# Layer 0 of a four-layer graph network: first product with seven products for eight, adjacency turned by whole groups, engine order from a table

## The chip, the core and the metric

The kernel runs on one core of a Trainium2 chip. A core has a matrix engine (TensorE, PE in the profile), a vector engine (VectorE, DVE), a scalar engine (ScalarE, ACT), a general engine (GpSimd, POOL) and a queue processor (SyncE, SP) that issues most DMAs. PE reads SBUF and writes the eight banks of PSUM. DVE and ACT move results from PSUM to SBUF. All data here are 32-bit floats. The metric is the device time of one execution in microseconds, as the median of several.

## What is computed

There are 128 graphs of 64 nodes with 256 features. Four layers follow one another, each with a residual sum and a normalisation over the features. Layer 0 is the part that the change rewrites:

```python
GROUPS = [list(range(25)), [0, 1, 2, 3, 4, 5, 6, 7, 8], [0, 9, 10, 11, 12, 13, 14],
          [6, 7, 8, 12, 13, 14], [3, 4, 5, 9, 10, 11]]

def _graph_conv(x, adj, W, b):
    A = adj + jnp.eye(n)
    deg = jnp.sum(A, axis=-1)
    dinv = jnp.where(deg == 0, 0.0, deg_safe ** (-0.5))
    norm_adj = dinv[:, :, None] * A * dinv[:, None, :]
    support = jnp.einsum('bnd,de->bne', x, W)
    out = jnp.einsum('bnm,bme->bne', norm_adj, support) + b
    return jax.nn.relu(out)

for g, idx in enumerate(GROUPS):
    h = _graph_conv(x[:, idx], adj[:, idx][:, :, idx], W1[g], b1[g])   # 256 -> 512 features
    out_g = _graph_conv(h, adj[:, idx][:, :, idx], W2[g], b2[g])       # 512 -> 256
    fused = fused.at[:, idx].add(norm_w[g] * out_g)
x = layernorm(x + fused)
```

Layers 1 and 2 are a graph convolution and a polynomial of the normalised adjacency. Layer 3 is a gated recurrent cell over five steps; it fills most of the run and the change leaves it as it is.

## The kernel before

Layer 0 is cut into 16 units. A unit holds up to four tiles; a tile holds the chosen nodes of so many graphs that its rows fit 128 partitions (14 graphs of group 1, 16 of group 2, 21 of groups 3 and 4, 5 of group 0). The groups come in the order 1, 2, 3, 4, 0: units 0 to 2, 3 and 4, 5 and 6, 7 and 8, 9 to 15. A full unit has 448 to 504 columns; the last of a group has fewer (144, 264, 264 and 200).

For each unit, in stages:

- `load0` loads `a` (rows of the adjacency) and `xg` (rows of x) for the unit, one DMA per tile and run of nodes.
- `prep` adds the identity, sums degrees, takes the root on POOL (`inv_sqrt`, a power instruction, L144), scales, spreads each row into a block-diagonal 126x126 matrix A0 (L467), has PE turn it into the bank pT (L475), and DVE scales the other side while it moves it to SBUF as AT (L480).
- `aggregate` multiplies xg by AT (pa, L492), and ACT copies the result to ag0 (L498).
- `hidden` is the first product: ag0 times W1 in four output blocks of 128, two matmuls each over the whole width of the unit (ph, L508), and four ReLUs on ACT (L512).
- `support` multiplies by W2, four matmuls of 256 columns a tile (ps, L524), copied by ACT.
- `add` multiplies by AT again (po, L546), ACT takes the ReLU with the group's weight (L550), and DVE adds the sum over groups: into F for groups 1 to 4, from F for group 0.
- `finish`, for group 0's units alone, has PE turn the sums back to rows (pse, L581), DVE adds them to xg (L586), normalises, and SP stores the rows.

The nodes outside group 0 (25 to 63) need only a normalisation; `others` does it for four nodes at a time in between. Layers 1 and 2 of the first two chunks of graphs (`mid`, a generator called `early`) are laid into the last turns of the loop by a list of places. Weights that layer 3 needs are loaded by POOL's queue at turn 4 (L750 to L760); their products, `folds` (L644), begin layer 3's preparation.

PE's order is the program order, written by hand through the loop over `i`, in which unit i's support, unit i+1's aggregate and first product, and unit i-1's add stand side by side. The order of the other engines in layer 0 is found by a scheduler, with hints (`issue_after`, `high_priority`). Banks of PSUM rotate through two pools of five and three. From layer 3 on, all engines follow hand-written order strings. There the gate products already use a scheme of seven products in place of eight (`Gates`): the two-by-two block product is made from seven half-width ones, with sums of the moving side taken on POOL (L817 to L819), a running bank that ACT copies between products (L857), and DVE additions from PSUM (L861).

Of the kernel before, what the change touches and what calls it, by code (L numbers as in the profile page):

```python
# [27 lines left out]
NP = CB // 2  # L28
# [36 lines left out]
WARM = 4  # L65

# [26 lines left out]
def gnn_stack(  # L93
# [305 lines left out]
    with ExitStack() as c0:  # L399
        w0 = c0.enter_context(tc.tile_pool(name="w0", bufs=1))  # L400
        work = c0.enter_context(tc.tile_pool(name="work0", bufs=1))
        W1 = w0.tile([128, NG, 2, HID], F32, name="W1")
        W2 = w0.tile([128, NG, 4, D], F32, name="W2")
# [6 lines left out]
        def load0(i, after=None):  # L410
# [5 lines left out]
            a = work.tile([TR, 4, NJ], F32, name="a", bufs=3)  # L416
            xg = work.tile([TR, 4, D], F32, name="xg", bufs=6)
# [7 lines left out]
            for rows, t, b, f in runs:  # L425
                qa[t % len(qa)].dma_start(a[rows, t, :w], adj[b, f, 0:w])
# [55 lines left out]

        def aggregate(i):
# [17 lines left out]
        def hidden(i):  # L501
# [3 lines left out]
            for e in range(4):  # L505
                p = psum0("ph")[:, : u.cols]
                for k in range(2):
                    nc.tensor.matmul(  # L508
                        p, W1[:, u.g, k, e * 128 : (e + 1) * 128], ag0[:, k, : u.cols], start=k == 0, stop=k == 1
                    )  # L510
# [4 lines left out]

        def support(i):
            u = UNITS[i]
            hg, s2 = HG.pop(i), []
            for v in range(0, len(u.tiles), 2):
                p = psum0("ps").rearrange("p (t d) -> p t d", t=2)  # L520
                ts = range(v, min(v + 2, len(u.tiles)))
                for t in ts:
                    for e in range(4):
                        nc.tensor.matmul(  # L524
                            p[: u.rows[t], t - v, :], hg[:, e, u.off[t] : u.off[t] + u.rows[t]], W2[:, u.g, e, :],
                            start=e == 0, stop=e == 3,
                        )
                sv = work.tile([TR, 2, D], F32, name="s2", bufs=4)
# [6 lines left out]
            S2[i] = s2  # L535

        def add(i):
# [4 lines left out]
            z = work.tile([128, 2, 512], F32, name="z", bufs=2)  # L542
            for k in range(2):
# [8 lines left out]
                )  # L552
            if u.g < 2:
# [16 lines left out]

        def finish(i):
# [3 lines left out]
            for v in range(0, len(u.tiles), 2):  # L575
                p = psum0("pse").rearrange("p (t d) -> p t d", t=2)
                ts = range(v, min(v + 2, len(u.tiles)))
                for t in ts:
                    r = u.rows[t]
                    for k in range(2):  # L580
                        nc.tensor.transpose(  # L581
                            p[:r, t - v, k * 128 : (k + 1) * 128], z[:, k, u.off[t] : u.off[t] + r], ident
                        )
                r = u.rows[v]
                if u.rows[ts[-1]] == r:
                    nc.vector.tensor_add(xg[:r, v : v + len(ts), :], p[:r, : len(ts), :], xg[:r, v : v + len(ts), :])  # L586
                else:
                    for t in ts:
                        r = u.rows[t]
                        nc.vector.tensor_add(xg[:r, t, :], p[:r, t - v, :], xg[:r, t, :])  # L590
            for ts, _, r, _ in u.same:
                layernorm(xg[:, ts], n=ts.stop - ts.start, r=r)
            for t, (b, nb) in enumerate(u.tiles):
                nc.sync.dma_start(xa[b // XP][b % XP : b % XP + nb], xg[: u.rows[t], t, :])
# [6 lines left out]

        def others(i):

            with tc.issue_after(evictions[-1].ins):
                layernorm(XO[i], n=XO[i].shape[1])

        def store_others(i):
            t = XO.pop(i)
            nc.sync.dma_start(xb[:, NP * i : NP * i + t.shape[1], :], t)

# [20 lines left out]
        def load_first(g):  # L631
            nc.sync.dma_start(W1[:, g], w1[g].rearrange("(k p) e -> p k e", p=128))

        def load_second(g):
            nc.sync.dma_start(W2[:, g], w2[g].rearrange("(k p) e -> p k e", p=128))

        load_first(1)

# [10 lines left out]
        early = both(mid(0, True), mid(1, True))  # L649

        places = [(1, 1), (1, 2), (2, 1), (2, 2), (2, 2), (3, 1), (3, 2), (3, 2)]
        places += [(4, 0), (4, 0), (4, 1), (4, 2), (4, 2), (5, 1), (5, 2), (5, 2)]

        def early_stage(i, place):
            for _ in range(places.count((i - g0, place))):
                next(early)
# [4 lines left out]

        g0 = next(i for i, u in enumerate(UNITS) if u.g == 0)
        for i in range(-2, NU + 1):
            if i >= 0:
                stage(load0, i + 3)
            stage(add, i - 1)
            if i:
                stage(aggregate, i + 1)
            early_stage(i, 0)
            stage(support, i)  # L670
            if not i:
                aggregate(1)
            if i == NU:
                folds = [products(0, q) for q in range(3)]
            stage(finish, i - 1, g0)
            early_stage(i, 1)
# [5 lines left out]
            else:  # L682
                stage(prep, i + 2)
                stage(hidden, i + 1)
            if i == -2:
# [4 lines left out]
                load0(2, powers[0])  # L690
                load_first(2)
            elif i == -1:
                load_second(2)
                load_first(3)
                for ks in (slice(3, 5), slice(0, 1)):
                    nc.sync.dma_start(block0[:, ks], c_block0[:, ks])
            elif i == 0:
                load_second(3)
            elif i < 5:
                (load_first, load_second)[(i - 1) % 2]((4, 0)[(i - 1) // 2])  # L700
            early_stage(i, 2)
            for f, j in ((store_others, i - 1), (others, i), (load_others, i + 2)):
                for o in range(10):
                    if min(o + 1, 9) == j:
                        f(o)
            if i == 0:

                with tc.issue_after(evictions[-1].ins):
                    nc.vector.memset(F, 0.0)
# [31 lines left out]
            elif i == 4:  # L741
# [6 lines left out]
                with tc.issue_after(powers[-1].ins):  # L748
                    for q in range(3):
                        nc.gpsimd.dma_start(ih[:, q], wihT[:, q * D : (q + 1) * D].rearrange("(k p) e -> p k e", p=128))  # L750
                    for l in range(L):
                        if l:
# [538 lines left out]
```

## Time and profile before

| what | us |
|---|---|
| median of 3 runs | 2125.28 |
| range of the runs | 2124.78 to 2125.33 |
| the profiled execution | 2125.68 |
| its span, first to last instruction | 2123.7 |
| PE busy in the span | 2102.9 |
| layer 0 (to the start of the folds) | 293.5 |
| folds and preparation of layer 3 | 32.5 |
| from the first gate product | 1797.7 |

The span is what the profile's instructions cover; the execution's own time is 2 us more. The page gives busy time by engine, the waits name who released an engine after idle time, the windows give the busy time of all engines in a stretch (columns: PE, PEld for weight loads, DVE, ACT, POOL, then the granted clock, the share of the DMA engines and GB/s), and the timeline gives start, length, engine, line and operation of merged runs of instructions. An fp32 matmul shows as two records, a transpose on PE as one.

### The profile page before, as it was taken

The page shows a single profiled execution, that of the slowest core. Times are in us where ns is not written, and L with a number is a line of the kernel's source. Part 1 is how long each engine was busy: PE and PEld are TensorE (multiplying, and loading weights), DVE is VectorE, ACT ScalarE, POOL GpSimd, SP SyncE. Part 2 cuts the span into 40 slices and gives each one's busy share as a digit, 9 for nine tenths or more (in the row PEclk, how much of TensorE's full clock was granted, in tenths as well). Part 3 has the DMA queues.
Part 4 walks back from the last instruction along what each step waited for, and adds up shares of the span by engine and source line. Part 5 has one row for each costly group of instructions (what it writes and reads, how often), then busy time and mean ns, then how long its engine had stood idle before and what let it go on. Part 6 is the DMA issues. An engine that isn't in the chain of part 4 may idle for free.

```text
span 2123.7 us, 31527 instructions
## 1 busy us (share of the span) xinstructions
PE 2102.9 (99%) x10738; PEld 1820.6 (86%) x10738; DVE 1661.1 (78%) x3849; ACT 978.9 (46%) x2006; POOL 594.8 (28%) x638
## 2 busy tenths in 40 slices
PE   9999999999999999999999999999999999999997
PEld 6777788888888888888888888888889888888886
DVE  3345666887988798788978898879887997888776
ACT  3333334445444454444544454445444454445453
POOL 3411122232323223222323332223232332223322
PEclk9999999999999999999999999999999999999999
DMA  6642110223321242223321342233312421233121
GB/s 167 178 135 63 33 44 21 55 60 75 85 70 41 68 97 65 50 56 80 90 54 40 75 100 59 56 72 79 80 41 60 95 75 40 60 65 93 47 56 40
DMA packets 522060, 149.81 MB, mean 71 GB/s; under 512 B 488734, under 2 KB 516924, under 8 KB 521900
## 3 DMA queue, kind: packets, MB, share of 16 engines
q1 hardware_dynamic: 516996, 142.58, 27.8%
q0 software_dynamic: 2192, 4.80, 1.0%
q8 instruction: 85, 1.39, 0.3%
q10 hardware_dynamic: 2712, 0.42, 0.1%
q14 instruction: 75, 0.61, 0.1%
HBM read 82.70 MB, written 65.01 MB: 70 GB/s over the span
## 4 chain that ended last, share of the span: by engine, by line
PE 86%; DVE 10%; issue 1%; DMA 1%; ACT 0%; SPq 0%; POOL 0%; DVEq 0%; POOLq 0%; ACTq 0%
PE parz L837 22%; PE pdrz L837 12%; PE pan L837 11%; PE pa L254 8%; PE pdn L837 5%; PE pbrz L837 5%; PE pd L333 5%; PE ps L524 5%; PE ph L508 4%; PE pbn L837 3%; DVE NI L995 1%; PE pa L492 1%; PE pp L314 1%; DVE NI L996 1%; PE po L546 1%
## 5 line engine op out<-in xcount | busy, mean ns | idle before, releaser
L938 ACT ACTIVATE RZ<-RZ,brz 128x256 f32<-128x256 f32 x474 | 214.7, 501 | 167.5 <-DVE RZ L861 166.8
L837 PE MATMUL parz<-Th,WHH 128*128 128x256 f32 x960 | 288.7, 382 | 3.1 <-ACT c L857 3.1
L817 POOL TENSOR_TENSOR Ta<-agg 128x512 f32<-128x512 f32 x80 | 103.7, 1296 | 662.4 <-ACT agg L256 662.3
L837 PE MATMUL parz<-Ta,V 128*128 128x256 f32 x960 | 285.5, 379 | 0.0
L857 ACT COPY c<-parz 128x512 f32<-128x512 f32 x240 | 139.0, 579 | 269.1 <-PE parz L837 268.2
L857 ACT COPY c<-pan 128x512 f32<-128x512 f32 x237 | 138.4, 584 | 183.9 <-PE pan L837 183.7
L953 ACT ACTIVATE NI<-NI,bih 128x256 f32<-128x256 f32 x316 | 149.2, 504 | 156.6 <-DVE NI L996 156.6
L837 PEld LDWEIGHTS parz<-Th,WHH 128*128 128x128 f32 x960 | 179.5, 190 | 35.5 <-ACT c L857 12.5
L837 PEld LDWEIGHTS parz<-Ta,V 128*128 128x128 f32 x960 | 182.4, 190 | 24.8
L170 POOL TENSOR_TENSOR rs<-ve,mhalf 128x4 f32<-128x4 f32 (+2 forms) x65 | 68.3, 1052 | 370.7 <-DVE ve L163 318.7
L817 POOL TENSOR_TENSOR Th<-hn 128x512 f32<-128x512 f32 x64 | 81.6, 1275 | 315.2 <-DVE hn L960 304.4
L958 DVE TENSOR_TENSOR RZ<-hn,NI 128x256 f32<-128x256 f32 x252 | 133.9, 532 | 34.8 <-ACT NI L953 34.4
L959 DVE TENSOR_TENSOR RZ<-RZ 128x256 f32<-128x256 f32 x316 | 150.9, 478 | 10.7
L861 DVE TENSOR_TENSOR NI<-pdn,c 128x512 f32<-128x512 f32 x158 | 108.1, 684 | 58.8 <-ACT c L857 55.3
L996 DVE TENSOR_TENSOR NI<-NI 128x256 f32<-128x256 f32 x237 | 137.9, 582 | 8.2
L837 PE MATMUL pan<-Ta,V 128*128 128x256 f32 x474 | 144.1, 385 | 0.2 <-ACT c L857 0.2
L837 PE MATMUL pan<-Th,WHH 128*128 128x256 f32 x474 | 141.0, 379 | 0.0
L861 DVE TENSOR_TENSOR RZ<-pdrz,c 128x512 f32<-128x512 f32 x160 | 109.6, 685 | 37.3 <-PE pdrz L837 26.0
L995 DVE SCALAR_TENSOR_TENSOR NI<-NI,bhh,RZ 128x256 f32<-128x256 f32 x237 | 129.1, 545 | 6.3 <-ACT RZ L938 1.4
L254 PEld LDWEIGHTS pa<-A,h 128*128 128x128 f32 x1024 | 124.5, 192 | 4.8 <-issue 1.5
L256 ACT COPY agg<-pa 128x512 f32<-128x512 f32 x160 | 93.6, 586 | 73.1 <-PE pa L254 72.2
L254 PE MATMUL pa<-A,h 128*128 128x128 f32 x1024 | 124.9, 275 | 1.4 <-DMA h<-hb 1.4
(228 smaller groups left out, 4716.8 us busy)
## 6 DMA issues: line engine op xcount, KB each, us to landing
hb<-flip SPq DMA_DIRECT2D x184, 256.0 KB
h<-hb SPq DMA_DIRECT2D x624, 64.0 KB
out_dram<-xt SPq DMA_DIRECT2D x30, 256.0 KB
hT<-hb SPq DMA_DIRECT2D x112, 64.0 KB
W<-in_w_dram SPq DMA_DIRECT2D x10, 512.0 KB
xt<-xb SPq DMA_DIRECT2D x32, 156.0 KB
xo<-in_x_dram SPq DMA_DIRECT2D x9, 512.0 KB
xb<-xo SPq DMA_DIRECT2D x9, 512.0 KB
```

What stands on the lines that cost most here:

```text
L254: nc.tensor.matmul(p[:, q * 128 : (q + 1) * 128], src(q, k), m[:, q, :], start=True, stop=True)
L333: nc.tensor.matmul(p[:, h, :], ag[:, k, q * 128 : (q + 1) * 128], W[:, k, :], start=k == 0, stop=k == 1)
L817: nc.gpsimd.tensor_sub(t[:, 0:2, :], a[:, :, H:], a[:, 0, :].rearrange("p (s n) -> p s n", s=2))
L837: nc.tensor.matmul(bank[:, g, :], w[:, q, i - 1, :], rhs, start=i in (1, 2, 5) and g == 0 and m == 0, stop=m == len(side) - 1, skip_group_ ...
L857: nc.scalar.copy(c, self.a)
L861: nc.vector.tensor_add(v, self.b if i == 2 else self.d, self.copies.pop({7: 7, 2: 1, 3: 6}[i]))
L938: nc.scalar.activation(v, self.g.a[:, q, :] if i == 4 else v, AF.Sigmoid, bias=brz[:, 2 * q + j : 2 * q + j + 1])
L953: nc.scalar.activation(n, n, AF.Tanh, bias=bih[:, 4 + j : 5 + j])
L958: nc.vector.tensor_sub(d, self.hT[:, j, f], n)
L959: nc.vector.tensor_mul(d, d, z)
L995: nc.vector.scalar_tensor_tensor(n[:, j, f], h, bhh[:, 4 + j : 5 + j], r[:, j, f], op0=ALU.add, op1=ALU.mult)
L996: nc.vector.tensor_add(n[:, j, f], i, n[:, j, f])
```

## The change

Seven things change, all in layer 0.

1. From unit 3 on, `hidden7` makes the first product with seven products of half the width for eight, as the gates do. `factors0` makes the sums of W1 on POOL, once per group; three sums of ag0 are made on POOL per unit; bank a is copied by ACT after products 1, 6 and 7; DVE adds copies to the banks b and d; ACT takes the ReLU in halves.
2. From unit 3 on, the adjacency is not turned by PE tile by tile. Whole graphs are loaded, 32 graphs on each of four bands of partitions; `norm_group` takes degrees and roots for a whole group, scales, turns 32x32 blocks with DVE, scales the other side and stores the result to DRAM; `load_turned` loads a unit's rows, and `spread_out` writes AT with one DVE product by the block mask.
3. For units 10 to 13 the sums are turned by DVE in 32x32 blocks (`turn_sum`), go through DRAM, and come back as rows (`finish_turned`).
4. The normalisations are cut into pieces (`pieces_of_norm`) that are called one by one.
5. From unit 2 on, ACT, DVE and POOL follow program order too, and the order of stages is a line of `ORDER0` per turn. Letters stand for stages (A aggregate, P add on PE, F the sum over groups, S a support tile, X spread, L loads, digits the seven products, b g d c their evictions, q a piece of what is waiting, e a piece of layers 1 and 2).
6. W1 and W2 are held for two groups at a time instead of all five, xg has five buffers instead of six.
7. Layer 3's weights are loaded three DMAs a turn from turn 5 on, instead of all at turn 4; F is cleared by POOL instead of DVE.

The core of the diff:

```diff
+ORDER0 = """
+P A S q L 1 X 2 F 6 5 q 7 g S q 4 d 3 b c S S
+A S 1 q q L q X q 2 5 q q 6 q S 7 P q S 4 q g q 3 q q S F b c d
+q q A L P 1 S q S 6 2 q X 5 q q q 7 S S g F q b 4 q q 3 d c
...
+        def norm_group(g):
+            n, o = len(GROUPS[g]), 0
+            S = AS[len(nts) % 2]
+            nts[g] = []
+            degrees(g)
+            deg, s, r = (roots[:, v, max(g - 1, 0)] for v in range(3))
+            nc.vector.scalar_tensor_tensor(s, deg, 0.0, deg, op0=ALU.is_equal, op1=ALU.add)
+            powers.append(nc.gpsimd.tensor_tensor(r, s, mhalf[:, :1].to_broadcast([128, 32]), ALU.pow))
+            for _ in range(WAITS):
+                yield
+            nc.vector.scalar_tensor_tensor(s, deg, 0.0, r, op0=ALU.not_equal, op1=ALU.mult)
+            d = s[:, :, None]
+            for f, m in RUNS[g]:
+                nc.vector.tensor_mul(S[:, :, f : f + m], AL[:, :, f : f + m], d.to_broadcast([128, 32, m]))
+            yield
+            nc.vector.transpose(AU.rearrange("p b n -> p (b n)"), S.rearrange("p b n -> p (b n)"))
+            yield
+            for f, m in RUNS[g]:
+                nc.vector.tensor_mul(S[:, :, o : o + m], AU[:, :, f : f + m], d.to_broadcast([128, 32, m]))
+                o += m
+            for f, m in RUNS[g]:
+                nt = dram.tile([B, m, n], F32, name=f"nt{g}{f}")
+                for v in range(4):
+                    nc.sync.dma_start(
+                        nt[32 * v : 32 * v + 32].rearrange("b j i -> j b i"), S[32 * v + f : 32 * v + f + m, :, :n]
+                    )
...
+                    with tc.high_priority():
+                        last = nc.vector.tensor_mul(
+                            AT[:r, ts, o : o + nb * m].rearrange("p t (b n) -> p t b n", n=m),
+                            a[:r, ts, None, c : c + m].to_broadcast([r, w, nb, m]),
+                            block0[:r, None, k, o : o + nb * m].rearrange("p t (b n) -> p t b n", n=m)
+                            .to_broadcast([r, w, nb, m]),
+                        )
...
+        def factors0(g):
+            w = work.tile([128, 4, 2, 128], F32, name="w7", bufs=2)
+            v = W1[g].rearrange("p k (u j e) -> p k j u e", u=2, j=2)
+            nc.gpsimd.tensor_add(w[:, 1], v[:, 0, 1], v[:, 1, 1])
+            nc.gpsimd.tensor_sub(w[:, 3], v[:, 0, 0], v[:, 0, 1])
+            nc.gpsimd.tensor_sub(w[:, 2], w[:, 1], v[:, 0, 0])
+            nc.gpsimd.tensor_sub(w[:, 0], v[:, 1, 0], w[:, 2])
...
+        def hidden7(i):
+            u = UNITS[i]
+            a = AG.pop(i)
+            c = u.cols // 2
+            t = work.tile([128, 4, 256], F32, name="t7", bufs=1)
+            nc.gpsimd.tensor_sub(t[:, 0:2, :c], a[:, :, c : 2 * c], a[:, 0, : 2 * c].rearrange("p (s n) -> p s n", s=2))
+            nc.gpsimd.tensor_sub(t[:, 2, :c], a[:, 1, c : 2 * c], t[:, 0, :c])
+            nc.gpsimd.tensor_sub(t[:, 3, :c], a[:, 1, :c], t[:, 2, :c])
...
+            def product(k):
+                n = {2: "b", 5: "d", 3: "d"}.get(k, "a")
+                if k in (1, 2, 5):
+                    banks[n] = psum0("ph")[:, : 2 * c].rearrange("p (u n) -> p u n", u=2)
...
+                for p in range(2):
+                    nc.tensor.matmul(
+                        banks[n][:, p, :], F7[u.g](k, p), rhs, start=k in (1, 2, 5) and p == 0, stop=p == 1,
+                        skip_group_check=True,
+                    )
+                if k in (1, 6, 7):
+                    copies[k] = work.tile([128, 2, 256], F32, name="c7", bufs=3)[:, :, :c]
+                    with tc.high_priority():
+                        nc.scalar.copy(copies[k], banks["a"])
+
+            def evict(k):
+                j, f, of = {2: (0, 0, 1), 7: (1, 1, 7), 4: (1, 0, 0), 3: (0, 1, 6)}[k]
+                o = hv[:, j, :, f * c : f * c + c]
+                if of:
+                    with tc.high_priority():
+                        nc.vector.tensor_add(o, banks["b" if k == 2 else "d"], copies.pop(of))
+                for p in range(2):
+                    e = u.g * 4 + 2 * p + j
+                    nc.scalar.activation(o[:, p], o[:, p] if of else banks["a"][:, p], AF.Relu, bias=b1[:, e : e + 1])
...
+        def turn_sum(i):
+            yield
+            z, xg = Z[i]
+            zt = work.tile([128, 2, 16, 32], F32, name="zt", bufs=1)
+            nc.vector.transpose(zt.rearrange("p k b f -> p (k b f)"), z.rearrange("p k c -> p (k c)"))
+            zd = dram.tile([512, D], F32, name="zd", bufs=2)
+            zv = zd.rearrange("(b n) (k w f) -> w n k b f", n=32, k=2, w=4)
+            for v in range(4):
+                nc.sync.dma_start(zv[v], zt[32 * v : 32 * v + 32])
+            zr = work.tile([TR, 4, D], F32, name="zr", bufs=1)
+            nc.sync.dma_start(zr[: u0], zd[: 4 * u0].rearrange("(t r) d -> r t d", r=u0))
...
+                with tc.issue_after(powers[0].ins):
+                    nc.gpsimd.memset(r2, 0.0)
+                    for v in range(4):
+                        b = slice(32 * v, 32 * v + 32)
+                        nc.gpsimd.dma_start(eye1[b], c_ident[b, b])
+                load_graphs(15, 15)
...
+                with tc.issue_after(powers[-1].ins):
+                    nc.gpsimd.memset(F, 0.0)
```

## Prediction, made before the changed kernel ran

> **What bounds the kernel now.** I read the page first: which engine has no idle time over the whole run.
>
> ```profile
> span 2123.7 us, 31527 instructions
> ...
> PE 2102.9 (99%) x10738; PEld 1820.6 (86%) x10738; DVE 1661.1 (78%) x3849; ACT 978.9 (46%) x2006; POOL 594.8 (28%) x638
> ```
>
> Only 20.8 us of the span are not PE's (2123.7 - 2102.9). A busy PE need not be a fast one, so next came the idle time by releaser (the waits of PE) and the stages (the windows).
>
> ```profile
> PE parz L837 <- ACT c L857: 3.1, 7, 1.5
> ...
> PE pT L475 <- DVE A L467: 1.1, 1, 1.1
> PE pa L492 <- DVE AT L480: 0.5, 1, 0.5
> ...
> PE ph L508 <- ACT ag L498: 0.2, 1, 0.2
> ```
>
> ```profile
> 0.00:150.00 150.00, 146.62 (x704) 107.22 (x704) 58.33 (x242) 53.20 (x92) 48.61 (x69) 1.00 0.59 166
> 150.00:293.50 143.50, 143.50 (x755) 113.24 (x755) 80.72 (x272) 51.89 (x88) 19.35 (x20) 1.00 0.15 46
> ```
>
> Layer 0 is the first 293.5 us. All PE idle time there is in the first 12 us (three lines of the waits and the start); after that PE is never idle, while DVE is busy 39% and 56% of the two windows, ACT 35% and 36%. The clock is full. So every microsecond of PE work taken out of layer 0 shortens the run until another engine or a transfer is late. The price of each piece of PE work is the distance from one start to the next in PE's timeline; here is one turn of the loop (first product and support of unit 11; pse of unit 9, po of unit 10, pT and pa of unit 12):
>
> ```profile
> 185.58 1.04 PE L581 MATMUL pse<-ident,z 128*125 128x128 f32 x8
> 186.45 0.60 PE L475 MATMUL pT<-ident,A 125*125 125x125 f32 x4
> 186.89 6.87 PE L508 MATMUL ph<-ag,W 128*128 128x500 f32 x16
> 193.60 1.95 PE L546 MATMUL po<-AT,s 125*128 125x125 f32 x16
> 195.38 1.95 PE L492 MATMUL pa<-AT,xg 125*128 125x125 f32 x16
> 197.17 7.07 PE L524 MATMUL ps<-W,hg 128*125 128x256 f32 x32
> ```
>
> Eight pse transposes take 0.87 us, four pT transposes 0.44, the eight matmuls of the first product 6.71 (each shows as two records), po and pa 1.78 each. A 256-column matmul takes 0.43 (the gate products later in the timeline start 0.43 apart), a 128-column one 0.22.
>
> [...] Here PEld is 86%, and the even spacing of starts shows PE really does stream, so I take start-to-start prices. [...] the records here say 272 ns, but the pitch in the stream is 0.11 us, and the pitch is what is saved. [...] the page's landing times here (3.3 to 7.0 us for POOL's) are longer, no short SP one is shown.
>
> **The change part by part: what leaves PE.**
> - First product, units 3 to 15: 8 matmuls of C columns become 14 of C/2, seven eighths of the columns. C=500 (six units): 6.71 - 14 x 0.422 = 0.80 each, 4.8 in all. C=448 (two): 6.02 - 14 x 0.378 = 0.73, 1.5. C=504 (two): 6.87 - 14 x 0.425 = 0.92, 1.8. C=264 (two): 3.56 - 14 x 0.231 = 0.33, 0.7. C=200: 2.71 - 14 x 0.175 = 0.26. Sum 9.0 us.
> - pT transposes of units 3 to 15 go (AT is now written by one DVE product from a loaded, already turned adjacency): the 13 pitches read from the timeline (0.38, 0.43, 0.43, 0.42, 0.43, 0.47, 0.44, 0.53, 0.44, 0.44, 0.49, 0.44, 0.22) sum to 5.6 us.
> - pse transposes of units 10 to 13: 4 x 0.87 = 3.5 us.
> PE loses 18.1 us.
>
> **What is added, and what covers it.**
> - ACT: three bank copies of C columns (0.58 each, as the gates' 128x512 copies) and eight half ReLUs for four whole ones (about 0.5 against 0.68): 3 us a unit. With 36% busy in a 17.5 us unit (6.3 us) it goes to about 9.5: covered.
> - DVE: three PSUM additions a unit (0.68 each, the gates' row): 2.1 us. The old A0 product (0.68), the AT eviction (0.68), ae, degree and scaling (about 1.1) leave, one spread product (0.68) comes: about equal. The turned sums add a 1024-column block transpose (0.69 for 512, so about 1.3) but replace PSUM by SBUF additions of the same length. DVE stays near 60%.
> - POOL: sums of the aggregate, 1.3 + 0.79 + 0.79 us (the gates' rows), so product 6 may start about 0.1 + 0.58 + 1.3 + 0.79 = 2.8 us after the aggregate's last matmul. The order puts po or a support tile (1.7) and products 1 and 2 (0.8 each) in between: 3.3 or more. Covered with half a microsecond.
> - Bank a is copied between products 1, 6, 7: the copy (0.58 and some 0.15 of hand-over) needs one other product (0.84) between; the order gives that or more. I take 0.5 us for all units, ends 0 and 2.
> - ACT, DVE and POOL are in written order from unit 2 on: one late instruction holds those behind it. For such mismatches, the layer-1 and -2 work of chunks 0 and 1 included, I take 1.5 us, ends 0 and 6.
> - DMA: the 'a' loads of units 3 to 15 (5632 short packets) become two loads of whole graphs (5120), the stores of turned groups (5632), their loads (5632), and 16384 packets of 128 bytes for the turned sums. About 27,000 more packets; at the mean of 18 ns of one engine (27.8% of 16 engines' span for 516996 packets) some 30 us of all sixteen, spread over 290. The share at 150 to 293 us is 0.15: covered. SP issues fewer loads of 'a' and so gets time back.
>
> **The start.** Unit 3's AT hangs on a chain: whole graphs loaded, degrees, a root on POOL, turn, 8 stores, 2 loads, spread. POOL is the narrow place:
>
> ```profile
> 11.57 1.03 POOL L144 TENSOR_TENSOR d0r<-d0s,mhalf 126x4 f32<-126x4 f32 x1 [0.67 <-DVE d0s L142]
> 20.51 1.05 POOL L144 TENSOR_TENSOR d0r<-d0s,mhalf 126x1 f32<-126x1 f32 x2 [7.91 <-DVE d0s L142]
> ...
> 34.18 0.55 POOL L727 MEMSET Ab<- 128x512 f32 x1
> ```
>
> In the instruction order of the new program a 2048-column memset (about 2.1 us at the memset's rate) and four small DMA issues (2.3) come ahead of unit 1's root, so it ends near 16.3 instead of 12.6; its transposes stand at 18.6 on PE: 1.2 us left. Unit 2's root comes after a 3840-column memset (3.8) and four factor sums (3.1) that wait for the second group's weights, so it ends near 27 instead of 21.6, and PE wants the transposes at 27.8: no slack. Then the root of 128x32: a root costs 0.55 us for one column and 1.0 for four, so 1.0 (flat) to 5.3 us (0.15 a column); I take 5.3. It ends near 32; DVE scales and turns until 36; SP, busy with x loads till about 35, issues 8 stores at 0.7 and waits for them till 43.5; the loads land near 47; unit 3's aggregate is wanted at 48.8. I charge 1 us for the start, ends 0 and 6.
>
> **The end of layer 0.** In the new PE order chunk 1's first product of layer 1 (pd) is followed by only two support tiles and po (5.2 us) before the gather of its normalised rows. The rows need the last 0.9 us of additions, statistics 2.3, a root 1.0, scaling 1.4 and hand-overs, about 6.2: 1 us of waiting. The gather's two copies are wanted at once by the second product: 0.7. The last unit's sums wait behind about 15 us of DVE norms: 1 us at the pse of unit 15, and 1 us more before the folds' bank additions (today DVE's delay there costs the 0.4 us that the waits put on L873). Sum 3.7 us, ends 0 and 6.
>
> **Sum.** -18.1 + 0.5 + 1.5 + 1 + 3.7 = -11.4 us. The profiled execution took 2125.7 (span 2123.7 and 2 around it), the median of the runs is 2125.28. So 2125.3 - 11.4 = 2113.9.
>
> **Rivals.** (A) All that is added is hidden, the start and the end included: -18 to -15, about 2109. For it: DVE, ACT and POOL have room; against: the two narrow places above. (B) The start and the tail both come late by what I bound (12 us): about -4, 2121. For it: DMA's share is 0.59 in the first 150 us and short packets rise. (C) Slower: the written order. DVE's spread product waits for a loaded adjacency, and the evictions of the running product stand behind it, so a round trip through DRAM that is late holds the banks and then PE, in each of 13 units. At 1.4 us a unit the 18 us are gone, at 1.7 the run is at 2129. Against: the store and load are issued one to two units (17 us each) ahead for all but units 3 and 4. (D) The change doesn't do what it says: the instruction order shows 14 half matmuls for units 3 to 15, so no.
>
> **How the numbers follow.** Likeliest, 2110.5 to 2118: 0.56. A: 0.14. B with what lies between (2118 to 2124): 0.16. C: 0.14. Forecast 2114. The range 2107.5 to 2123 leaves out most of C and a little of both ends. 0.2% is 4.3 us, what a measurement here can tell: faster than 2121.0 has 0.56 + 0.14 + about 0.09 = 0.79, within 2121.0 to 2129.5 about 0.09, slower 0.12.
>
> **What would show it.** After: no pT records past unit 2, 20 pse transposes instead of 52, first-product groups of 5.9 us; layer 0's end (the first gate product, now 325.9) near 314; PE waits of about 1 us at unit 2 or 3's aggregate, and at pa, pd and pse before the folds; the gate part unchanged at 1798 us. Wrong if PE waits show in most units (C), if the root of 32 columns is much over 5.3, or if the gate part moves.

## The result and the profile after

The changed kernel took 2151.78 us (median of 4 runs, 2147.78 to 2154.35), the kernel before 2125.03 beside it on the same chip: a ratio of 1.0124, 95% interval 1.0107 to 1.0142. It is 26.7 us slower, where 11 us less was forecast. The profiled execution took 2147.78 us, so it is the fastest of the four and understates the loss by 4 us. Its page shows this:

```profile
span 2146.0 us, 31812 instructions
...
PE 2099.1 (98%) x10814; PEld 1843.2 (86%) x10814; DVE 1705.3 (79%) x3825; ACT 1001.0 (47%) x2097; POOL 653.6 (30%) x693
```

PE's idle time, span less busy, has grown from 20.8 to 46.9 us. PE's own waits, by what ended them (us in total, times, longest), name the places:

```profile
PE ph L651 <- DVE hg L665: 8.5, 2, 7.3
PE ph L651 <- POOL t L635: 8.0, 1, 8.0
PE pse L778 <- DVE z L725: 4.0, 1, 4.0
PE pa L272 <- DVE V L1136: 3.2, 1, 3.2
```

None of these four was there before, when the longest wait of PE in layer 0 was 1.5 us. By windows (columns: the stretch and its length, busy time of PE, weight load, DVE, ACT and POOL with counts, granted clock, DMA share, GB/s), layer 0 and then all the rest:

```profile
0.00:150.00 150.00, 138.50 (x725) 112.98 (x726) 83.93 (x235) 61.02 (x132) 87.59 (x94) 0.97 0.61 159
150.00:307.70 157.70, 143.88 (x811) 127.07 (x810) 92.49 (x244) 68.19 (x140) 38.37 (x50) 0.96 0.30 77
307.70:2146.00 1838.30, 1816.71 (x9282) 1603.10 (x9281) 1528.88 (x3347) 871.81 (x1826) 527.63 (x550) 1.00 0.28 65
```

The first fold starts at 307.73 instead of 293.54 and the first gate product at 346.66 instead of 325.86, 20.8 us later; from there to the end it is 1799.3 us against 1797.8. So the loss lies in layer 0 and its end. Two things are new in the first two rows: PE is not full, and the granted clock is under 1.00 with DVE at about 57% and DMA no more than 0.61.

To split the 20.8 us I went through PE's records of the first 360 us and summed two things: the idle time before each (the 1.5 us ahead of the first record not counted), and by how much the distance to the next start exceeds the median distance of the same form, idle time taken off ("stretched"). Before: 2.3 idle and 2.6 stretched. Since the clock was full throughout that stretch before, the measure is no sharper than these 2.6 us. After: 27.0 and 14.8. That is 24.7 + 12.2 = 36.9 us of new loss. With 20.8 us seen, 36.9 - 20.8 = 16.1 us of PE work have gone, where the prediction took out 18.1. So most of the work did go; more than twice as much came back.

**The work that went.** One turn in PE's timeline, the first product of unit 5 as seven pairs of half matmuls among the support tiles of unit 4:

```profile
75.35 1.95 PE L590 MATMUL pa<-AT,xg 126*128 126x126 f32 x16
77.13 1.94 PE L711 MATMUL po<-AT,s 112*128 112x112 f32 x16
78.91 1.03 PE L651 MATMUL ph<-ag,W 128*128 128x252 f32 x4
...
90.93 1.01 PE L651 MATMUL ph<-ag,w 128*128 128x252 f32 x4
91.78 0.39 PE L590 MATMUL pa<-AT,xg 126*128 126x126 f32 x2
```

From one pa to the next it is 16.43 us, against 17.76 for the same turn before: 1.33 less, and the prediction's terms for this turn (0.92 for the product, 0.43 for pT) sum to 1.35. The counts agree too (matmuls on one tile: line, count, shortest, median and longest ns, first and last start); pT had 58 records and pse 52:

```profile
L492 PE MATMUL pT<-ident,A x10: 181/271/326, 8.1 to 27.8; 126*126 126x126 f32 x9, 18*18 18x18 f32 x1
```

```profile
L778 PE MATMUL pse<-ident,z x20: 272/273/375, 186.4 to 315.6; 128*125 128x128 f32 x18, 128*75 128x128 f32 x2
```

**First place: group 0's adjacency, 8.0 us.** The timeline of four engines (start, length, engine, line, operation; in brackets the idle time before and what ended it):

```profile
109.76 14.56 SPq L541 DMA_DIRECT2D nt<-AU  x4
...
129.88 0.68 DVE L571 TENSOR_TENSOR AT<-a,block 125x500 f32<-125x500 f32 x1 [7.56 <-DMA a<-nt]
...
130.06 2.27 POOL L1040 DMA_DIRECT2D wl<-in_wlT_dram  x3 [10.34 <-DMA a<-nt]
132.35 0.73 POOL L620 TENSOR_TENSOR w<-W 128x256 f32<-128x256 f32 x1
...
136.01 0.46 POOL L635 TENSOR_TENSOR t<-ag,t 128x132 f32<-128x132 f32 x1
...
136.53 1.25 PE L651 MATMUL ph<-t,w 128*128 128x132 f32 x4 [8.00 <-POOL t L635]
137.57 1.09 PE L651 MATMUL ph<-ag,W 128*128 128x132 f32 x4
138.45 3.33 PE L685 MATMUL ps<-W,hg 128*126 128x256 f32 x8
```

SP needs 14.56 us to issue the four stores of the turned adjacency. They begin at 109.8, DVE wants the rows of unit 9 at 122.3, and the load of them lands at 129.9. POOL's weight load (part 7) overwrites the memory the turning used and, by the profile, waits for the same load; behind it in POOL's order stand the four factor sums and the aggregate's differences, and behind those PE. The list of waits names only the last link, "POOL t"; POOL itself had been idle for 10.34 us, for a DMA, ahead of the weight loads that come before these sums; the aggregate that the sums read had been copied by ACT at 124.0, and they start at 135.2. Then the last line: four matmuls of 256 columns (eight records) take 3.33 us, where the same four take 1.89 elsewhere.

**Second place: the turned sums, 7.3 us.**

```profile
242.62 3.23 SPq L748 DMA_DIRECT2D zd<-zt  x3
...
248.08 0.26 SPq L750 DMA_DIRECT2D zr<-zd  x1
...
254.63 1.29 DVE L759 TENSOR_TENSOR xg<-zr,xg 125x512 f32<-125x512 f32 x2 [8.26 <-DMA zr<-zd]
...
260.77 0.67 DVE L665 TENSOR_TENSOR hg<-ph,c 128x500 f32<-128x500 f32 x1
...
261.50 2.04 PE L651 MATMUL ph<-ag,w 128*128 128x250 f32 x4 [7.29 <-DVE hg L665]
```

Three of the four stores go out at 242.62, the load at 248.08, and DVE comes to the addition at 246.4 and stands for 8.26 us. The eviction that PE needs is behind it, and behind some 5 us of statistics and scaling. The stores are late because SP, in order too, first waits for one of the five xg buffers (3.7 us, the x load of unit 15 at 240.94). DVE waits four times for zr, 19.4 us in all; one of the four becomes a long wait of PE.

**The clock.** The same window view, over each of these two places:

```profile
125.00:150.00 25.00, 17.00 (x90) 15.06 (x89) 10.62 (x35) 5.96 (x17) 12.01 (x16) 0.80 0.58 158
250.00:275.00 25.00, 17.70 (x92) 15.52 (x91) 15.12 (x41) 8.08 (x18) 3.70 (x6) 0.80 0.35 82
```

0.80 over 25 us is 10 us at half speed. In the record of granted clock of the changed kernel there are four stretches at 0.5 ahead of the first gate product (10.2, 10.2, 6.8 and 3.4 us; a window over each gives 0.50), and none in the kernel before, where the window from 0 to 325.8 gives 1.00. They begin 2.6, 3.2, 5.1 and 2.9 us after a wait of PE began, and run on for 4.8, 6.1, 7.9 and 3.1 us after PE has work again. PE was at work in 20.2 us of these 30.6, so 10.1 us are lost to the clock, most of the 12.2 "stretched". Whether the wait is the cause here was tried by itself, below.

### The profile page after: what moved, and what is told of

Read it like the earlier page. It is cut to its first block, busy times and chain, and to the rows that moved or that the text cites. A ratio compares the mean times of both kernels' runs of the same rounds, so it can differ in the third digit from the quotient of the medians.

```text
span 2146.0 us, 31812 instructions
## 1 busy us (share of the span) xinstructions
PE 2099.1 (98%) x10814; PEld 1843.2 (86%) x10814; DVE 1705.3 (79%) x3825; ACT 1001.0 (47%) x2097; POOL 653.6 (30%) x693
## 4 chain that ended last, share of the span: by engine, by line
PE 79%; DVE 12%; DMA 4%; SPq 2%; issue 1%; POOL 1%; ACT 0%; DVEq 0%; POOLq 0%; ACTq 0%
PE parz L1168 22%; PE pdrz L1168 11%; PE pan L1168 11%; PE pa L272 8%; PE pdn L1168 5%; PE pbrz L1168 5%; PE pd L351 5%; PE ps L685 3%; PE pbn L1168 3%; PE ph L651 2%; DMA zr<-zd 1%; DVE NI L1326 1%; PE pp L332 1%; PE pf L881 1%; DVE NI L1327 1%
```

## The experiments

The theory was: *three in-order queues (SP, POOL, DVE), each with a wait on a DRAM round trip in it, hold evictions and factors, and PE pays each wait again at half clock.* The main rivals: the seven half products themselves don't pay; the written order is the fault; the end of layer 0 is too long for DVE. No run undoes part 2 (the turned adjacency), so what it costs or saves as a whole is not shown. All runs in one table; before was 2124.8 to 2125.0 beside each. Idle and stretched as above, first 360 us.

| run | median us | ratio (95%) | idle | stretched | first gate product |
|---|---|---|---|---|---|
| before | 2125.03 | 1 | 2.3 | 2.6 | 325.86 |
| after | 2151.78 | 1.0124 (1.0107-1.0142) | 27.0 | 14.8 | 346.66 |
| e1_moves_later | 2142.28 | 1.0082 (1.0067-1.0097) | 20.8 | 16.2 | 342.71 |
| e2_pe_turn | 2132.87 | 1.0040 (1.0026-1.0054) | 16.3 | 9.6 | 334.39 |
| e3_both | 2129.55 | 1.0023 (1.0016-1.0031) | 14.1 | 9.8 | 332.15 |
| e4_xg6 | 2139.43 | 1.0072 (1.0057-1.0087) | 22.5 | 10.2 | 339.15 |
| e5_seven_alone | 2168.30 | 1.0204 (1.0186-1.0222) | 37.7 | 17.0 | 367.62 |
| e6_whole | 2130.04 | 1.0027 (1.0017-1.0036) | 9.1 | 4.6 | 330.22 |
| e7_sched | 2148.43 | 1.0116 (1.0099-1.0133) | 27.1 | 13.1 | 348.45 |
| e8_tail | 2131.25 | 1.0032 (1.0019-1.0045) | 15.5 | 6.3 | 329.82 |
| e9_three | 2129.18 | 1.0019 (1.0010-1.0028) | 14.5 | 9.2 | 331.90 |
| e10_whole_tail | 2131.01 | 1.0028 (1.0018-1.0039) | 10.3 | 6.4 | 333.12 |
| e11_pause | 2134.65 | 1.0047 (1.0032-1.0062) | 9.3 | 5.5 | 335.86 |
| e12_start | 2131.34 | 1.0032 (1.0022-1.0043) | 10.5 | 10.6 | 329.21 |
| e13_both_ends | 2144.51 | 1.0094 (1.0079-1.0109) | 27.1 | 11.8 | 346.99 |

**e1: POOL's weight loads one turn later** (part 7).

```
-            if i > 4:
+            if i > 5:
...
-                    for m in moves[3 * (i - 5) : 3 * (i - 4)]:
+                    for m in moves[3 * (i - 6) : 3 * (i - 5)]:
```

> Layer 3's weight loads start on POOL's queue one turn later (turn 6 instead of 5); nothing else changes. Theory Q (a DMA issue at the head of POOL's in-order queue waits for the turned adjacency of group 0 and holds the sums of unit 8 behind it): the 8.0 us wait of PE for the sums at L635 goes, with the half-clock stretch after it (about 2.5 us), so about 10 us less than the changed kernel, near 2141. Rival D (DVE's own wait for the same load holds the banks anyway): the wait moves from POOL's sums to DVE's evictions of unit 8, and at most 4 us are won. Rival S (the seven-product scheme costs PE time everywhere): no gain.

9.5 us less than the changed kernel. The waits of PE now read:

```profile
PE ph L651 <- DVE hg L665: 8.6, 2, 6.6
PE ph L651 <- ACT c L658: 3.7, 1, 3.7
```

POOL is out of the list. At the same place 3.7 us stay, under another name: DVE's spread product still waits 7.1 us for the turned adjacency; an eviction stands behind it on DVE, a ReLU of ACT waits for that eviction, and the bank copy stands behind the ReLU. The second place is untouched.

**e2: group 0's sums transposed by PE again** (part 3 undone, 3.5 us of PE work put back).

```
-            if g0 < i - 2 < NU - 2:
-                fill.append(finish_turned(i - 2))
-            if i - 1 in (g0, NU - 2, NU - 1):
+            if i - 1 >= g0:
                 fill.append(finish(i - 1))
-            elif g0 < i - 1 < NU - 2:
-                fill.append(turn_sum(i - 1))
...
         def finish(i):
...
+            while i not in Z:
+                yield
```

> The sums of units 10 to 13 are turned by PE again, as those of units 9, 14 and 15 are; the way through DRAM goes, and 32 transposes (3.5 us) come back. Theory Q (DVE stands 19.4 us at the head of its queue for rows on their way back through DRAM, and evictions stand behind): the PE waits of 7.3, 1.2 and most of 4.0 us go with their half-clock stretches (about 8 us), less the 3.5: 15 us less than the changed kernel, near 2136. Rival S (DVE is simply full at the end of layer 0): the waits at the folds stay and the time moves by less than 5 us.

18.9 us less, the largest of any single part, although PE does 3.5 us more. The zr waits are gone, the 7.2 us behind POOL remain:

```profile
PE ph L651 <- POOL t L635: 7.2, 1, 7.2
PE pse L780 <- DVE z L725: 4.6, 2, 4.2
```

**e3: both edits together.**

> Both edits. If both waits are real and independent the gains add: 10 + 15, near 2127 less what was hidden behind either, so 2115 to 2127. If the first product and the turned adjacency are worth what the sum of the prediction says (14.6 us without the turned sums), it ends near 2113 to 2116. Rival S: above the kernel before by 10 us or more.

22.2 us of the 26.7 are back, but the forecast gain isn't: 2129.55 lies above the numbers of both theories and below the rival's. One by one the two edits gave 9.5 + 18.9 = 28.4, so 6.2 us of that are shared or lost again elsewhere. What is left of PE's waits is spread over small ones:

```profile
PE pse L780 <- DVE z L725: 4.6, 2, 4.2
PE pa L590 <- issue: 3.2, 1, 3.2
PE pd L351 <- DVE poly L341: 1.9, 1, 1.9
...
PE ph L651 <- ACT c L658: 1.4, 1, 1.4
```

**e4: six xg buffers instead of five** (part 6 undone in that point; A0 shares zt's memory), all else as changed.

```
-            xg = work.tile([TR, 4, D], F32, name="xg", bufs=5)
+            xg = work.tile([TR, 4, D], F32, name="xg", bufs=6)
```

> xg has six buffers again, as in the kernel before (the block-diagonal buffer shares a place with the buffer of the turned sums to make room). Theory X (the x load of unit 15 waits for the store of unit 10's rows, which holds three of the four stores of unit 11's turned sums behind it in SP's queue for 4 us): the 7.3 us wait shrinks by about 4, so 4 to 6 us less than the changed kernel. Rival (the way through DRAM is too long by itself): less than 2 us.

12.4 us less, twice what the theory said. Idle time fell by 4.5 us (table), about what it said; stretched work fell by another 4.6. PE's waits for an eviction are now

```profile
PE ph L652 <- DVE hg L666: 5.3, 2, 3.2
```

The longest went from 7.3 to 3.2, so the buffer that SP waited for was about half of the lateness at the second place; the rest is the round trip.

**e5: the kernel before with the seven half products alone.** Its PE order is written for units 3 to 15; ACT, DVE and POOL are left to the scheduler; the weights come two groups at a time.

```
+                product, evict = hidden7(i + 1)
+                sup = supports(i)
+                for o in "S12S65bS7gS4d":
...
+                stage(prep, i + 2)
+                product(3)
+                evict(3)
```

> The kernel before with part 1 of the change alone (units 3 to 15 make their first product as seven half products; adjacency, sums and engine order stay as before). Theory 'the PE work taken out is real, the losses come from the DRAM round trips of parts 2 and 3 in front of evictions on in-order queues': no new DRAM round trip here, so most of the 9.0 us of the first product is kept, 2116 to 2120, PE idle in layer 0 under 5 us. Rival 'the seven-for-eight form itself does not pay, because its bank copies, additions and factor sums on ACT, DVE and POOL hold the products': 2124 to 2130, with waits of PE on the copies of bank a, on the factor sums and on the half evictions in most units.

43 us slower than before, worse than either theory said. The waits of PE (and the first of POOL's) show why it doesn't settle the matter:

```profile
PE ph L552 <- POOL t L536: 20.0, 4, 11.8
PE ph L552 <- ACT c L559: 9.6, 9, 2.7
```

```profile
POOL w L521 <- DMA W<-in_w_dram: 38.2, 3, 16.3
```

Two of the four waits for POOL, 11.8 and 5.3 us, follow a group's weights that land late, which is this kernel's loading and not the product. But nine waits for a bank copy are the form itself, in 7 of the 13 units: with one product between a bank's copy and its next use, ACT must be there within about 0.85 us (one product in the turn above), and with the scheduler's order it often isn't.

**e6: e3 with the first product whole again** (part 1 undone).

```
-P A S q L 1 X 2 F 6 5 q 7 g S q 4 d 3 b c S S
...
+P A S q L X F q S q H S S
...
```

> The kernel e3_both with the first product whole again (part 1 of the change undone, its steps left out of the written order). It shows what the seven half products are worth inside the new structure. Theory 'the half products save their 9.0 us there too': e3_both plus 7 to 9 us, 2137 to 2139. Rival 'what the half products save is lost again at waits of in-order queues (the AT product that waits for its load, the factor sums)': within 3 us of e3_both, 2127 to 2133, with the wait of PE on the factor sums or on bank copies gone.

The rival was right: 2130.0 against e3's 2129.6, with overlapping intervals. In this structure the half products are worth nothing in the time. Where their 9.0 us go is less certain. By the table e6 waits 5.0 us less and is stretched 5.2 us less, but its profile is the fastest of its ten runs (2127.12), e3's lies above its median (2130.77), and 3.2 us of the waits are one at the start (see e12) that e3's profile has and e6's hasn't.

**e7: e3 with ACT, DVE and POOL left to the scheduler** (part 5 undone).

```
-            if i == 2:
-                written.enter_context(tc.manual_schedule(engines=free))
```

> The kernel e3_both with the orders of ACT, DVE and POOL left to the scheduler (part 5 of the change undone; PE's order stays written). Theory 'a written order fixes each late instruction in front of the evictions, and this is the main remaining loss': e3_both minus 5 to 12 us, 2118 to 2125. Rival 'the order is not the matter; the scheduler puts the long DVE work ahead of evictions at least as often': e3_both or more, 2129 to 2145, with more DVE and ACT waits of PE in layer 0.

18.9 us slower than e3: the written order isn't the fault; against what the scheduler finds around the same order of PE, it is worth that much. Its list of waits is that of e5, copies (8.7 us), factors (3.8) and evictions (2.4), beside 7.1 us at the start.

**e8, e9, e10: the end of layer 0.** In e3 the last four pse stand at 302.95 behind 4.24 us of idle, because unit 15's addition into F comes on DVE after unit 14's norm. e8 makes that norm wait:

```
+            while i == NU - 2 and NU - 1 not in Z:
+                yield
             for ts, _, r, _ in u.same:
```

e9 adds two moves in the written order (turn 8: the spread product behind the evictions; turn 14: a step of layer 1 ahead of a norm); e10 is e8 with the whole product.

> The kernel e3_both with one edit: the norms of unit 14's sums wait until unit 15's sums are emitted, so that on DVE (whose order is the written one) the last addition into F no longer stands behind some 6 us of statistics and scaling. Theory 'DVE's in-order queue holds the last transposes pse by 4.2 us': the wait of PE for z falls below 1 us, the clock stretch behind it goes, and the run is 4 to 7 us under e3_both, 2122 to 2126. Rival 'the end of layer 0 is bound by the number of DVE instructions, and the wait only moves to the folds (V) or to the first gate product': same wait at pa <- V, 2127 to 2130.

> The kernel e8_tail with two more edits of the written order: in turn 8 the AT product that waits for the turned adjacency of group 0 stands behind that turn's evictions instead of ahead of them, and in turn 14 a step of layer 1 stands ahead of four pieces of a norm. Theory 'every wait left is one late instruction ahead of others on DVE, and all that the change was to bring comes when none is left': 2 to 5 us under e8_tail, 2116 to 2121, faster than the kernel before. Rival 'the waits move to the next place': within 1.5 us of e8_tail, with new waits of PE of the same sum.

> The kernel e6_whole (first product whole) with the edit of e8_tail alone. It is the partner of e8_tail: theory 'with the waits gone the half products are worth their 9.0 us': e8_tail 3 to 9 us under this one, this one 2125 to 2128. Rival 'the half products cost about what they save': both within 2 us.

None comes near what its theory said (2122 to 2126, 2116 to 2121, and 3 to 9 us between e8 and e10): the rivals held in kind, though e8 and e9 lie up to 1.3 us outside their numbers. In e8 the 4.2 us at pse became these:

```profile
PE pa L272 <- DVE V L1136: 4.2, 1, 4.2
PE pf L885 <- DVE xg L790: 2.7, 1, 2.7
```

From chunk 1's layer-1 sums to the folds DVE has a chain of some 30 us (275.05 to 305.37 in e9), with gaps only where it waits for PE, ACT or a root on POOL; in the kernel before the same chain runs from 266.64 to 302.67. What differs is PE: before, it has 26.9 us of other work between the chain's start and the first fold (293.54), in e9 15.2 (to 290.23), and so it comes to the folds' results before DVE does. The order alone doesn't fix the wait at V: e12 has e9's order there, and its wait at V is 0.2 us against 2.6. In after and e9 the first two operations of DVE on V (V<-V, 128x384) take 1.5 to 1.6 us each, in before and e3 0.5 to 0.6. What slows them was not looked for.

Of e9's two other moves, the one in turn 14 removed the wait at pd (1.9 us). The one in turn 8 missed the wait it was meant for (2.1 us, against 1.5 in e8): it moves the spread product of unit 10, which waits for nothing in e8, while the one that stands 5.5 us for its load in e9 is that of unit 9, in turn 7, whose line is unchanged. So a spread product of group 0 that stands behind the evictions was not tried. e8 and e10 are again equal (2131.25 and 2131.01), with half and with whole products.

**e11: is it the wait that halves the clock?** The kernel before, with POOL multiplying an aggregate by one ahead of the first product in two units:

```
+            for _ in range({6: 8, 11: 12}.get(i, 0)):
+                v = ag0[:, 0, : u.cols]
+                nc.gpsimd.tensor_mul(v, v, one[:, :1].to_broadcast([128, u.cols]))
             AG[i] = ag0
```

> The kernel before with two waits put in by hand: POOL multiplies the aggregate of unit 6 by one 8 times (about 10 us) and that of unit 11 12 times (about 15 us) ahead of the first product, of which some 8 us lie beside other PE work; so PE should wait about 2 to 3 us and about 7 us. The result of the computation does not change. Theory 'a wait of PE makes the clock of TensorE halve for some us afterwards, whatever caused the wait': each is followed by a stretch with the granted clock at 0.5 and matmuls of twice their length, and the run is longer than before by 1.5 to 2 times the waits, 14 to 20 us. Rival 'the half clock in the changed kernel comes from its own work (more small matmuls, more copies), not from the waits': longer by the waits alone, 9 to 10 us, clock 1.0 throughout.

In unit 6 other PE work hid all of it, and the clock stayed full there; in unit 11 PE waited. Timeline, then the window over it:

```profile
186.20 0.60 PE L477 MATMUL pT<-ident,A 125*125 125x125 f32 x4
193.93 9.83 PE L513 MATMUL ph<-ag,W 128*128 128x500 f32 x16 [7.13 <-POOL ag L503]
```

```profile
175.00:200.00 25.00, 17.87 (x85) 13.38 (x84) 19.91 (x45) 5.51 (x9) 17.66 (x17) 0.80 0.26 71
```

The same first product took 6.87 us before. The wait cost 7.1 and the stretch behind it 3.0; the run is 9.7 us longer. The clock was at 0.5 from 189.5 to 199.7, that is, from 2.7 us into the wait until 5.8 us after it: half of 5.8 is the 2.9 lost. So the wait is the cause, and its price here is 1.4 times its length, less than the 1.5 to 2 of the theory. The 9.7 us fall on the rival's 9 to 10 by chance: they are one wait and its half clock, not two waits at full clock. No other work of the change is needed to explain the half clock, and POOL's multiplications in unit 6, without a wait of PE, brought none.

**e12, e13: both ends once more.** The start first: in e3, e8 and e9 PE waited 2.0 to 3.4 us, and in e7 7.1, for unit 3's turned adjacency near 48 us, as SP issued the eight x loads of unit 5 (6.5 us) ahead of the stores. In e3, e8 and e9 SP began these stores at 39.5 to 41.4 us; in after, e1, e2 and e6, which have the loads in the same place and no such wait, at 38.1 to 38.4. e12 puts the loads behind; e13 also pulls three steps of layer 1 forward in turn 13 and puts unit 15's norm ahead of unit 14's.

```
-                        stage(load0, i + 3)
+                        with tc.issue_after(turns_of[0]) if i == 2 else nullcontext():
+                            stage(load0, i + 3)
```

> The kernel e9_three with its start alone changed: on SP the eight x loads of unit 5 (6.5 us of issues, wanted at about 80 us) and the first gate adjacency stand behind the stores and loads that turn group 2's adjacency, instead of ahead of them. Theory 'the 2 to 7 us for which PE waits at unit 3's aggregate near 48 us is SP's order in front of the turned adjacency': that wait and the half clock behind it go, 4 to 6 us under e9_three, 2123 to 2125. Rival 'the chain root, turn, stores, loads is itself too long for the shorter turns': the wait stays within 1 us of what it was, 2128 to 2130.

> e12_start with the end changed too: three steps of layer 1 stand earlier in turn 13, and on DVE unit 15's sums and norm stand ahead of unit 14's norm. Theory 'DVE's queue in the last 30 us is the last of the lost gain': the waits of PE at pf and pa (2.7 and 2.6 us in e9_three) fall under 2 us together, and the run is 4 to 8 us under e12_start, 2116 to 2120, faster than the kernel before. Rival 'DVE has too much work between unit 14's product and the folds whatever its order': waits of the same sum at other instructions, within 2 us of e12_start.

In e12 the stores begin at 33.0 and the wait at the start is gone, so the rival is out; but PE waits one unit later, for factors on POOL, which sat idle for 4.67 us for their weights to land, and the run is 2.2 us slower than e9 instead of 4 to 6 faster:

```profile
PE ph L652 <- POOL t L635: 3.0, 1, 3.0
PE pf L886 <- DVE xg L791: 2.7, 1, 2.7
PE ph L652 <- ACT c L659: 2.6, 1, 2.6
```

e13 made it worse by 13 us, which neither of its forecasts said. DVE's layer-1 scaling now stands behind the statistics of another sum, and the folds' V behind three norms, one after another (309.9 to 319.5):

```profile
PE pa L272 <- DVE V L1142: 9.8, 1, 9.8
PE pa L272 <- DVE xt L203: 7.1, 1, 7.1
```

No version beat the kernel before. The best, e9, is 0.2% slower (interval 0.1 to 0.3%).

## Why the prediction was wrong, step by step

- **What leaves PE (18.1 us): right, within about 2 us.** The turn above agrees to 0.02 us and the counts are those forecast; in the whole of layer 0, 16.1 us are traced. The gate part was to stay at 1798 us and is 1799.3; the root of 128x32 was taken at 5.3 us and took 5.42.
- **The step that failed is the cover of the DRAM round trips: rival C's "Against", and a term that was put at nothing.** C's "Against" said that store and load are issued one to two units (17 us each) ahead "for all but units 3 and 4". For group 0's adjacency the stores began 12.6 us ahead of where DVE wanted the rows (109.8 against 122.3), less than one unit, and issuing the four took 14.56 us. For the turned sums the sum of the prediction has no round trip at all: it takes off 3.5 us of PE work and calls DVE and DMA covered. Here store, load and addition stood in one turn (stores at 242.6, load at 248.1, DVE there at 246.4), and DVE waited 19.4 us in four places. Undoing part 3 alone gave 18.9 us. C named the way it happens, evictions behind a DVE instruction that waits for DRAM; it was priced "in each of 13 units", where it struck in two places with 7 to 8 us each, the second at an addition that C does not name. C was given 0.14 and 2129 us; 2151.8 is far beyond it, and C's own sign, waits in most units, did not appear. That blocks turned by DVE have to go through DRAM was not shown; no run tried another way for them.
- **"Mismatches of the written order", 1.5 us, ends 0 and 6, was mis-sized.** The two waits at DVE and POOL are 15.3 us of idle PE by themselves, over twice the upper end. The written order isn't bad in itself (e7); it has no slack for a transfer that is late.
- **DMA, "the share is 0.15: covered", used the wrong measure.** The share of the engines' time was indeed low (0.30 after, in the second half of layer 0), as DVE's was (it stayed near 60%, as said). What ran out was the issuing queue: SP's order, with its own waits for buffers and earlier transfers. The prediction counted packets and not what stands behind what on SP and POOL. It also had landing times in hand (the page's list runs from 2.1 us for 16 KB to 7.0, not from 3.3) and charged them to the start alone. Part 7's weight loads were never given a step at all, and are worth 9.5 us (e1).
- **A term is missing: the clock.** Every wait was charged at its length. Of the 36.9 us, 10.1 are lost by work at half clock after waits (e11 shows the cause).
- **The first product's 9.0 us were counted as saved time.** Inside the new structure they are worth 0 (e3 against e6, e8 against e10). "Every microsecond of PE work taken out of layer 0 shortens the run until another engine or a transfer is late" was the right sentence; something was late at once. That it is DVE's chain at the end and SP's order at the start is argued from the waits in e3 to e13; no run without both was reached.
- **The start (1 us) was 0 in the profiled execution,** but 2.0 to 3.4 us in e3, e8 and e9, within the ends given, and 7.1 in e7, above them; the half clock comes on top. **The end (3.7 us)** measured 4.0 + 3.2 = 7.2, a little over its end of 6, with half clock after it.

What adds up: undoing part 3 and moving part 7 bring back 22.2 of the 26.7 us. The other 4.5, and the 14.6 us less PE work that should have made e3 faster than the kernel before, are open: the waits that e3 shows are at the start, at group 0's round trip and at DVE's end chain, but no run removed them together. Whether a version exists in which that work becomes time is open too.

## What to carry to other kernels

When an engine that works in its written order gets an instruction that waits for a DRAM round trip (here POOL stood for 10.34 us and DVE for 8.26), look up on each queue (the issuing one too) when the store is issued, not when it is written in the program, and list what stands behind the waiting instruction. Price a wait of several us of a full TensorE at more than its length: about 1.4 times here, as an estimate (9.7 us for a wait of 7.1 in e11; 10.1 us lost to the clock beside 24.7 us of new waits in the changed kernel). Before taking work out of the busy engine, find the chain on the next engine that ends at the same point, and where in the busy engine's order it starts: if it was hidden by just that work (26.9 us before, 15.2 in e9, for a chain of some 30), what is taken out may not become time.

## What the runs showed of the hardware

- In the changed kernel, ahead of the first gate product, the four longest waits of PE were each followed by a stretch of granted clock 0.5: 8.0 us (from 128.5; 10.2 us at 0.5 from 131.1), 7.3 (from 254.2; 10.2 from 257.4), 4.0 (from 300.1; 6.8 from 305.2) and 3.2 (from 322.8; 3.4 from 325.7). In e11 it was a wait of 7.1 us (from 186.8; 10.2 from 189.5). In the kernel before, whose longest wait there was 1.5 us, the clock was 1.00. After a wait of 1.9 us at pd, the next eight records of pd took 3.11 us in e3 and 1.97 in e2; what decides between them was not tried.
- Four stores of the turned 25-node adjacency, rows of 25 floats (78 KB each), took SP 14.56 us to issue in the changed kernel; eight smaller ones (turned group 2) took 4.21.
- The runs of one kernel spread differently: before's sets over 0.8 to 3.2 us, e3's 15 runs over 7.3 (2126.67 to 2134.01), e11's four, with the wait of 7.1 us, over 1.3. The wait at the start of layer 0, which was 0 in some profiles (after, e1, e2, e4) and 2.0 to 3.4 us in others of the same order there (e3, e8, e9), is one place where e3's spread may come from; that was not traced further.
